# Moving the position terms into the q and k projection of a four-layer kernel, with earlier loads and an in-place norm

## The chip, the cores and the metric

The program runs on one core of a Trainium2 chip. The metric is the device time of one execution in microseconds; three runs of the kernel before are at hand, and one more execution was profiled. In what follows PE is the matmul engine, PEld its weight loads, DVE, ACT and POOL are the vector, scalar and general engines, and SP is the engine that issues most of the DMAs. A queue name such as SPq or ACTq means the issuing of a DMA by that engine.

## What is computed

The input is an image of 48 x 48 tokens with 768 channels, float32, and four layers follow each other. The first is an attention block with position terms:

```python
xn = layernorm(x)                                   # 2304 tokens, 768 channels
q, k, v = split(xn @ qkv_w + qkv_b)                 # 12 heads of 64
attn = (q * 64**-0.5) @ k.T
attn += rel_h[q_row, k_row] + rel_w[q_col, k_col]   # rel_h = q @ Rh(row), rel_w = q @ Rw(col)
x = x + softmax(attn) @ v @ proj_w + proj_b
x = x + gelu(layernorm(x) @ mlp_w1 + b1) @ mlp_w2 + b2
```

Layers two and four are spectral: a real 2-D Fourier transform, a two-layer block-diagonal complex network with soft shrinkage over the spectrum, the inverse transform, and the residual. Layer three is a scan: projections of the tokens give decay, angles and inputs, then 12 iterations of a depthwise 3 x 3 convolution of a state of 64 x 4 channels with injection, and an output projection with silu.

## The kernel before, in words

All matmuls are float32 except the position products, which use sums of three bf16 parts. The tokens are cut into six blocks of 384 (`TB`), two of which make a superblock `sb`; there are three. The large products are done with seven block products in place of eight (`combine`, `block_sums`, `rows_in_seven`).

The program is written in one order, and a scheduler reorders the instructions of each engine before the launch: an instruction later in the program may be put ahead when its inputs and buffers are ready in the scheduler's own timing. [...] A tile pool with `bufs=n` has n buffers of a tag; a new tile waits until a buffer is free. A pool that closes gives its space to later pools.

**qkv_phase (L181 to L461).** For each superblock: `prepare` norms two blocks of three 128-token tiles (`layernorm_rows`, L62, its last step at L84 into a tile `ln_xh`) and transposes them (L93) with copies by ACT and DVE (L95, L97) into `xnT`; `v_rows` computes v (L164); `q_and_k` goes over six pairs of heads `pr`, seven products each (L293), stores q and k through ACT's queue (L323) and reduces their maxima (L324). `load_qk` (L244) loads the pair's weights. `position_terms` gives 24 steps per superblock: 12 `rel_w` steps (L390) and 12 `rel_h` steps (L410), four matmuls each on a table `relD` that SP loads (L374), and a split into three bf16 parts by ACT and DVE in turn (L366 to L369). The results lie in the one tile `rw` and the one tile `rh`, 16 and 24 rows at a time are stored with six DMAs (L398) and, per block, four (L417). The steps of a superblock run between the products of the next superblock's v (`between`); those of the last one run after `ahead()`, that is after the loads of the first keys (L494), the first q chunk (L505) with its eight position loads (L472, L474), and the one-hot matrix (L480).

**attention_bounded (L514 to L615).** 36 chunks: six head pairs times six blocks of queries. In groups of three key tiles PE computes q-k products (L546), adds the position terms with the one-hot matrix (L554); ACT takes the exponential into tiles `p` (L556, nine buffers); DVE adds them up in `acc` (L561, L564); PE multiplies with the values (L575) one group later. `finish` sums `acc` over the keys with PE (L583), takes the reciprocal (L585) and scales (L586) with DVE. Every seventh group `weight_sums` (L721 onwards) does a piece of preparing later weights: loads into `p` tiles, sums on POOL, and stores (`second`, L752: the sums go to a tile of their own). Loads for the next chunk and pair are issued by SP.

**proj_phase, mlp_phase (L690, L772).** The projection and the MLP in seven products; rows of the norm are prepared within them. `follow` (L1474) takes each finished block of rows (half 0 or half 1 of the channels), loads it, transforms it (L1322) and stores it to `yu`; the last blocks are done after the last product with `last=True`.

**afno_first, scan_phase, afno_second.** `spectrum_mix` walks over 40 items (half, five columns, block) in four stages with a delay (L1380, L1394 to L1396, L1415/L1416, L1430); it begins with half 1. Then the inverse along the other axis, `f_w` (L1518). The scan's projections (L1061) run with activations (L1069 to L1081) and DVE work (L1089 to L1120) per three token columns; then 11 iterations over eight groups of channels (L1150 to L1170). At the end each group's product with the turned c (L1176, POOL) goes to the transposes (L1212). `afno_second` is the second spectral layer; its last loop (L1549 to L1552) adds the residual and stores the output through ACT's queue.

Of the kernel before, what the change touches and what calls it, by code (L numbers as in the profile page):

```python
# [11 lines left out]
F32 = mybir.dt.float32  # L12
# [7 lines left out]
P = 128  # L20
G = 48
# [40 lines left out]
def layernorm_rows(nc, pool, xt, name):  # L62
# [20 lines left out]
    xh = pool.tile([P, C], F32, tag="ln_xh", name=f"{name}_xh")  # L83
    nc.vector.tensor_scalar(xh, xt, mv[:, 0:1], r, ALU.subtract, ALU.mult)  # L84
    return xh
# [38 lines left out]
TERMS = ("T1", "T2", "T3", "T4")  # L124
# [56 lines left out]
def qkv_phase(tc, ident, x, qkv_w, qkv_b, relT, rel_d, ln_g, ln_b, q_d, k_d, v_d, rw_d, rh_d, wqk_d, wv_d, flag, ahead):  # L181
# [17 lines left out]
    with (  # L199
# [11 lines left out]
        def load_x(sb, half):  # L211
            for t in range(3):
                i = (2 * sb + half) * 3 + t
                Xs[i] = xp.tile([P, C], F32, tag="x", name=f"x_{i}", bufs=4)
                nc.sync.dma_start(Xs[i], x[i * P : (i + 1) * P, :])

        def prepare(sb, half):

            blk = 2 * sb + half
            if half == 0:  # L220
                ops[sb] = kp.tile([P, NC, 2, TB], F32, tag="xnT", name=f"xnT_{sb}", bufs=2)
# [45 lines left out]
        def q_and_k(sb):  # L267
            tok = slice(sb * TS, (sb + 1) * TS)
            q = qp.tile([P, NC, 2, TB], F32, tag="q", name=f"q_{sb}")
            made = []  # L270
            for pr in range(NC):
# [18 lines left out]
                for n in range(7):  # L290
# [28 lines left out]
                    else:  # L319
                        k_out(0, u)  # L320
                for o, d, m in ((q[:, pr], q_d, qms), (kt, k_d, kms)):
                    o = o.rearrange("p b t -> p (b t)")
                    nc.scalar.dma_start(d[pr * P : (pr + 1) * P, tok], o)  # L323
                    V.tensor_reduce(m[:, pr, sb : sb + 1], o, axis=AX.X, op=ALU.max, apply_absolute_value=True)  # L324
                if pr == NC2 and sb + 1 < NSB:
                    prepare(sb + 1, 0)
                    load_x(sb + 1, 1)
# [4 lines left out]
            return q  # L332
# [26 lines left out]
        with tc.tile_pool(name="qkv_o", bufs=1, side="right") as op:  # L359
            R = HD + G  # L360
# [16 lines left out]
            def position_terms(sb, q):  # L377

                q6 = q.rearrange("p c b (j w h) -> p c b j w h", j=KJ, w=KTW)
                rw = op.tile([P, 3, NC, TS], BF16, tag="rw", name=f"rw_{sb}")  # L380
                ds = {}

                def rel_w(g):

                    d = tables(1, g, sb)
# [5 lines left out]
                    at = rw.rearrange("p s c (b t) -> p s c b t", b=2)  # L391
                    cols = slice(j * P + w0 * KTH, j * P + (w0 + 4) * KTH)
                    split(ps[:R, :TB].rearrange("p (c b t) -> p c b t", c=NC, b=2), [at[:R, n, :, :, cols] for n in range(3)], f"w{sb}_{g}")
                    if g == G // 4 - 1:
                        for s in range(2):
                            for j in range(KJ):
                                r0 = s * HD + j * KTW
                                nc.sync.dma_start(rw_d[s, j, :, :, sb].rearrange("n w f -> w n f"), rw[r0 : r0 + KTW].rearrange("w n c t -> w n (c t)"))  # L398

                def rel_h(n, cp, hh):  # L400

                    blk = 2 * sb + n
                    if cp == 0:
                        ds[hh] = tables(0, 2 * blk + hh, 0)
                        if hh == 0:
                            ds["at"] = op.tile([P, 3, NC, TB], BF16, tag="rh", name=f"rh_{blk}")
                    ps = pm.tile([P, 512], F32, tag="m", name=f"rh_{blk}_{cp}_{hh}")
                    for i in range(4):
                        rhs = q6[:, 2 * cp : 2 * cp + 2, n, :, :, 4 * hh + i].rearrange("p c j w -> p c (j w)")
                        nc.tensor.matmul(ps[:R, i * 2 * G : (i + 1) * 2 * G], lhsT=ds[hh][:, i, :], rhs=rhs, start=True, stop=True)  # L410
                    at = ds["at"][:, :, 2 * cp : 2 * cp + 2].rearrange("p s c (w h) -> p s c w h", h=KTH)
                    split(ps[:R, :TB].rearrange("p (h c w) -> p c w h", h=4, c=2), [at[:R, k, :, :, 4 * hh : 4 * hh + 4] for k in range(3)], f"h{blk}_{cp}_{hh}")
                    if hh == 1 and cp == NC // 2 - 1:
                        for s in range(2):
                            for half in range(2):
                                r0 = s * HD + half * G // 2
# [1248 lines left out]
```

## Time and profile before

| what | value |
|---|---|
| median of three runs | 3935.67 us (3929.7 to 3935.88) |
| the profiled execution | 3932.65 us |
| its span, first to last instruction | 3930.7 us |
| granted TensorE clock, mean | 0.971 |
| PE busy / PEld | 3773.9 us (96%) / 2301.0 us |
| DVE / ACT / POOL busy | 2066.0 / 1116.4 / 649.0 us |
| moved by DMA | 457.24 MB, mean 116 GB/s |

By stages, with the time in which PE had a matmul:

| stretch (us) | what | PE busy | granted clock |
|---|---|---|---|
| 0 to 43 | first norm, first v | 23.2 | 0.88 |
| 43 to 468 | v, q and k, position terms | 420.0 | 0.99 |
| 468 to 553 | last position terms, first products of attention | 42.0 | 0.77 |
| 553 to 1730 | attention | 1163.7 | 1.00 |
| 1730 to 1864 | projection, norm | 129.6 | 0.98 |
| 1864 to 2881 | MLP | 1016.6 | 1.00 |
| 2881 to 2904 | between MLP and spectral layer | 5.0 | 0.61 |
| 2904 to 3163 | first spectral layer | 251.3 | 0.96, then 0.51 |
| 3163 to 3571 | scan | 394.5 | 0.98 |
| 3571 to 3652 | output of the scan | 71.4 | 0.74, then 0.97 |
| 3652 to 3931 | second spectral layer | 256.7 | 0.96, then 0.88 |

How to read it: the page of a profile gives the busy time of each engine, then the span in 40 equal slices (a digit is the busy share in tenths; PEclk is the clock granted to the matmul engine), the chain of work that ended last, and the costliest groups of instructions. A line of the chain in order of time is: start in us, duration in us, what. A line of the waits is: who waited, for whom, us in total, times, longest. A line of the timeline is: start, duration, engine, line of the kernel, operation, output and inputs with shapes, count, and in brackets the idle time before it and what ended it. A line of the windows is: the stretch, its length, busy time of PE, PEld, DVE, ACT and POOL with counts, the granted clock, the DMA share and GB/s. Float32 matmuls appear as two records each. Matmul ends are modelled in the profile.

### The profile page before, as it was taken

To read this page: it belongs to the slowest core of one execution; us is meant where nothing else is said; L and a number is where in the kernel's file an instruction comes from. 1 tells how busy PE (TensorE), PEld (TensorE's weight loads), DVE (VectorE), ACT (ScalarE), POOL (GpSimd) and SP (SyncE) were. 2 spreads that over 40 slices of the span, in tenths; PEclk is the share of its full clock that TensorE was granted. 3 is DMA by queue.
4 is the path that set the end of the run, shared out by engine and by line. 5 is a ranking of instruction groups with operands and counts; after the bars stand their busy time and mean duration, and the time that the engine had idled before them with its cause. 6 is when DMAs were issued, how large, how long until landed. Compare 5 with 4: busy or idle time off the path is not lost.

```text
span 3930.7 us, 54207 instructions
## 1 busy us (share of the span) xinstructions
PE 3773.9 (96%) x22018; PEld 2301.0 (59%) x22018; DVE 2066.0 (53%) x3184; ACT 1116.4 (28%) x1888; POOL 649.0 (17%) x497
## 2 busy tenths in 40 slices
PE   7999879999999999999999999999979998999998
PEld 4666544444444444445555555555558876996685
DVE  6645446666666666565425333232325357995345
ACT  1323234444444444420310120021013235222341
POOL 3101001011010101024000000000013210981131
PEclk9999989999999999999999999999989789999999
DMA  7666463333232322124334433533434302110444
GB/s 252 191 190 187 160 176 106 100 105 114 95 105 81 113 73 89 57 77 158 132 106 145 156 109 120 157 114 107 150 106 104 98 25 95 36 36 22 143 106 157
DMA packets 262426, 457.24 MB, mean 116 GB/s; under 512 B 32413, under 2 KB 215701, under 8 KB 255799
## 3 DMA queue, kind: packets, MB, share of 16 engines
q1 hardware_dynamic: 251927, 431.07, 36.1%
q10 hardware_dynamic: 10240, 22.61, 1.5%
q8 instruction: 175, 2.87, 0.3%
q14 instruction: 84, 0.69, 0.1%
HBM read 315.31 MB, written 138.31 MB: 115 GB/s over the span
## 4 chain that ended last, share of the span: by engine, by line
PE 81%; DVE 8%; DMA 4%; POOL 2%; issue 2%; ACT 2%; SPq 1%; ACTq 0%; DVEq 0%; POOLq 0%
PE p L845 12%; PE p L908 12%; PE av L575 10%; PE s L546 10%; PE qk L293 6%; PE s L554 4%; PE c L1061 4%; PE pj L164 3%; PE v L164 3%; DVE rec L585 2%; PE f_z L1415 2%; PE f_z L1416 2%; PE f_x L1380 2%; PE f_u L1430 2%; PE so L1221 2%
## 5 line engine op out<-in xcount | busy, mean ns | idle before, releaser
L564 DVE TENSOR_TENSOR acc<-acc,p 128x768 f32<-128x768 f32 x576 | 585.0, 1016 | 355.7 <-ACT p L556 314.0
L556 ACT ACTIVATE p<-s 128x768 f32<-128x768 f32 x648 | 478.4, 811 | 707.3 <-PE s L554 707.3
L546 PE MATMUL s<-qt,kt 64*128 64x384 f32 x2592 | 479.3, 502 | 22.5 <-DVE rest_h L367 21.1
L908 PE MATMUL p<-w,h 128*128 128x384 f32 x1512 | 492.4, 486 | 0.0
L575 PE MATMUL av<-p,vt 128*64 128x384 f32 x2592 | 467.4, 496 | 17.2 <-DVE oT L586 11.2
L908 PEld LDWEIGHTS p<-w,h 128*128 128x128 f32 x1512 | 286.4, 190 | 196.6
L546 PEld LDWEIGHTS s<-qt,kt 64*128 64x128 f32 x2592 | 233.7, 187 | 264.2 <-ACT p L556 88.2
L575 PEld LDWEIGHTS av<-p,vt 128*64 128x64 f32 x2592 | 172.2, 137 | 238.8 <-issue 194.0
L845 PE MATMUL p<-x2nT,w 128*128 128x384 f32 x864 | 293.8, 490 | 0.5 <-issue 0.5
L1150 PE MATMUL c<-H,bands 128*48 128x96 f32 x5632 | 242.6, 247 | 12.5 <-issue 12.3
L554 PE MATMUL s<-bt,oneh 120*128 120x384 bf16 x1296 | 248.7, 328 | 0.0
L1150 PEld LDWEIGHTS c<-H,bands 128*48 128x48 f32 x5632 | 235.5, 124 | 19.8 <-issue 12.7
L293 PE MATMUL qk<-xnT,wqk 128*128 128x384 f32 x756 | 244.8, 486 | 0.0
L845 PEld LDWEIGHTS p<-x2nT,w 128*128 128x128 f32 x864 | 165.4, 192 | 116.4 <-issue 3.2
L845 PE MATMUL p<-xT,w 128*128 128x384 f32 x648 | 220.8, 486 | 0.0
L554 PEld LDWEIGHTS <-oneh 120*128 120x128 bf16 x1296 | 109.3, 98 | 174.4 <-issue 113.2
L293 PEld LDWEIGHTS qk<-xnT,wqk 128*128 128x128 f32 x756 | 143.5, 190 | 99.3
L884 POOL TENSOR_TENSOR rr<-rr,ml_b 128x1152 f32<-128x1152 f32 x12 | 32.0, 2668 | 955.3 <-DMA rr<-xr_d 742.1
L840 ACT ACTIVATE h<-h,ml_b 128x384 f32<-128x384 f32 x144 | 88.4, 614 | 348.9 <-DVE h L860 176.6
L845 PEld LDWEIGHTS p<-xT,w 128*128 128x128 f32 x648 | 123.2, 190 | 85.8
L1158 POOL TENSOR_TENSOR t<-s,c 128x768 f32<-128x768 f32 x80 | 144.7, 1835 | 172.5 <-DMA bands<-in_bands_dram 160.6
L1061 PE MATMUL c<-wsc,x2T 128*112 128x357 f32 (+1 forms) x576 | 151.9, 427 | 2.0 <-DVE c L1022 2.0
(301 smaller groups left out, 4766.6 us busy)
## 6 DMA issues: line engine op xcount, KB each, us to landing
w<-w1s_d SPq DMA_DIRECT2D x36, 768.0 KB
w<-w2s_d SPq DMA_DIRECT2D x36, 768.0 KB
bt<-rh_d SPq DMA_DIRECT2D x144, 162.0 KB
w<-w1s_d SPq DMA_DIRECT2D x36, 576.0 KB
w<-in_mlp_w_dram SPq DMA_DIRECT2D x27, 768.0 KB
wqk<-wqk_d SPq DMA_DIRECT2D x12, 1344.0 KB
f_gt<-yu SPq DMA_DIRECT2D x24, 672.0 KB
bt<-rw_d SPq DMA_DIRECT2D x144, 108.0 KB
```

Source lines behind the costliest of these rows:

```text
L164: nc.tensor.matmul(p[:, :TB], lhsT=rhs[n][:, c, t * P : (t + 1) * P], rhs=w[:, c, :], start=c == 0, stop=c == NC2 - 1)
L293: nc.tensor.matmul(p[:, :TB], lhsT=w[:, n, c, :], rhs=ops[sb][n][:, c, :], start=c == 0, stop=c == NC2 - 1)
L546: nc.tensor.matmul(ps[:, s, :QB], lhsT=keys[pr][rows, kt * P : (kt + 1) * P], rhs=chunks[c][0][rows], start=True, stop=False)
L554: nc.tensor.matmul(ps[:, s, :QB], lhsT=oneh[:NBR, b % 3, :], rhs=chunks[c][1][:NBR, s, b // 3, j, :], start=False, stop=True)
L556: nc.scalar.activation(p, ps[:, :, :QB], AF.Exp)
L564: nc.vector.tensor_tensor(probs[c], probs[c], p, ALU.add)
L575: nc.tensor.matmul(avs[c][rows, :QB], lhsT=vals[pr][:, kt, rows], rhs=p[:, s, :], start=kt == 0, stop=kt == NT - 1)
L845: nc.tensor.matmul(p[:, :TB], lhsT=w[n][:, c, :], rhs=rhs[n][:, c, :], start=c == 0, stop=c == NC2 - 1)
L908: nc.tensor.matmul(ps[t][:, :TB], lhsT=hs[left, f][:, t * P : (t + 1) * P], rhs=wt[:, f % KW2, :], start=f == 0, stop=f == NF2 - 1)
L1061: nc.tensor.matmul(ps[:K, i, :n], lhsT=xT[:, cc, tok : tok + K], rhs=w[:, cc, c0 : c0 + n], start=cc == 0, stop=cc == NC - 1)
L1150: nc.tensor.matmul(ps[r0 : r0 + G, k // 4, cols], lhsT=bands[:, n - GC, i, :] if gr else bands0[:, n, i, :], rhs=H[:, n, :, d : d + NPR], ...
L1158: GP.tensor_tensor(t, sc[:, ch], c1[:, m0 : m0 + GC].unsqueeze(2).to_broadcast([P, GC, RR, NPR]), ALU.mult)
```

## The change

It has these parts.

1. The position steps come in another order, `rel_h` by pairs of q tiles first, and are called within the next products of the same superblock: two per pair `pr` from the third pair on (eight of 24), the rest between the products of the next v; in the last superblock four run after the bound and twelve after `ahead(1)`. Tables are loaded up to three steps ahead. The tables have 96 columns instead of 112, `rh` holds two q tiles for a superblock, and the stores are two DMAs per tile of 48 rows each.
2. Normed activations and keys with values share one pool `home`. The first keys and values and the one-hot matrix are loaded within the last superblock's q and k (`ahead(0)`), the first chunk where all loads stood before (`ahead(1)`).
3. `layernorm_rows` writes into its input; the x tiles have six buffers.
4. Attention: row sums and reciprocal are issued before the last group's values; ten `p` buffers; the sums of `second` are done in place and stored with two DMAs.
5. Rows of the spectral transform: the last MLP product has two calls of `follow`; the last block's rows are done in steps 1 and 4 of `spectrum_mix`.
6. The scan's activations come in another order; the last group's final product runs on DVE; the last output group of each half is stored in four DMAs on two queues; `gt` has three buffers.

```diff
-    xh = pool.tile([P, C], F32, tag="ln_xh", name=f"{name}_xh")
-    nc.vector.tensor_scalar(xh, xt, mv[:, 0:1], r, ALU.subtract, ALU.mult)
-    return xh
+    nc.vector.tensor_scalar(xt, xt, mv[:, 0:1], r, ALU.subtract, ALU.mult)
+    return xt
...
-                Xs[i] = xp.tile([P, C], F32, tag="x", name=f"x_{i}", bufs=4)
+                Xs[i] = xp.tile([P, C], F32, tag="x", name=f"x_{i}", bufs=6)
...
-                ops[sb] = kp.tile([P, NC, 2, TB], F32, tag="xnT", name=f"xnT_{sb}", bufs=2)
+                ops[sb] = home.tile([P, NC * TS], F32, tag="xn", name=f"xnT_{sb}").rearrange("p (c n t) -> p c n t", c=NC, n=2)
...
+                    if pr > 1 and n in (2, 5):
+                        step()
...
+                if pr == 1 and sb + 1 == NSB:
+                    ahead(0)
...
-            R = HD + G
+            R = 2 * G
...
+                def store(d, at, cols):
+                    for s in range(2):
+                        nc.sync.dma_start(d[s, :, :, sb, cols], at[s * G : (s + 1) * G].rearrange("k n c b t -> k n (c b t)"))
...
+                        tiles["rh"] = op.tile([P, 3, 2, 2, TB], BF16, tag="rh", name=f"rh_{sb}_{cp}")
...
+            def advance():
+                while len(ready) < 3 and steps:
+                    load, run = steps.pop(0)
+                    load()
+                    ready.append(run)
+                if ready:
+                    ready.pop(0)()
...
+            for _ in range(4):
+                advance()
             inner.close()
-            ahead()
-            for step in steps:
-                step()
+            ahead(1)
+            while steps or ready:
+                advance()
...
+    def keys_values(kv, pr):
+        nc.sync.dma_start(kv[:, :T], k_d[pr * P : (pr + 1) * P, :])
+        nc.sync.dma_start(kv[:, T:].rearrange("p (t c) -> p t c", t=NT), v_d[:, :, pr * P : (pr + 1) * P])
...
-        tc.tile_pool(name="at_q", bufs=2) as qp,
-        tc.tile_pool(name="at_p", bufs=9) as pp,
+        tc.tile_pool(name="at_p", bufs=10) as pp,
...
                 c, k0 = work[i - 1]
+                if k0 + KB == NT:
+                    row_sums(c)
                 for kt in range(k0, k0 + KB):
                     values(c, kt)
                 if k0 + KB == NT:
...
-            rhs = block_sums(nc, X, *(xp.tile([P, NC2, TB], F32, tag=f"x{n}", name=f"pj_x{n}_{sb}") for n in ("T1", "T2", "T4")))
+            rhs = block_sums(nc, X, *(sp.tile([P, NC2, TB], F32, tag=f"x{n}", name=f"pj_x{n}_{sb}") for n in ("T1", "T2", "T4")))
...
-        combine_right(nc.gpsimd, [i[n // 2][:, n % 2] for n in range(4)], *(o[:, n] for n in range(4)))
+        b11, b12, b21, b22 = (i[n // 2][:, n % 2] for n in range(4))
+        combine_right(nc.gpsimd, (b11, b12, b21, b22), b11, b22, b12, b21)
         yield
-        nc.sync.dma_start(w2s_d[:, :, f, :].rearrange("n p c -> p n c"), o)
+        for h in range(2):
+            nc.sync.dma_start(w2s_d[2 * h : 2 * h + 2, :, f, :].rearrange("n p c -> p n c"), i[h])
...
-                xt = xp.tile([P, C], F32, tag="x", name=f"ml_x_{blk}_{t}")
+                xt = xp.tile([P, C], F32, tag="x", name=f"ml_x_{blk}_{t}", bufs=6)
...
-                    if f == NF2 // 2:
+
+                    if f in ((3, 9) if (sb, n) == (NTB // 2 - 1, 6) else (6,)):
                         follow(psum)
...
-        follow(psum, last=True)
...
-                    nc.scalar.activation(ga, za[:, NA - 1 : NA, :], AF.Sigmoid)
-                    nc.scalar.activation(alq, za[:, NCR : NCR + NN, :], AF.Sigmoid)
+                    for t in (g, x):
+                        nc.scalar.activation(t, t, AF.Silu)
...
-                    for t in (c, x, g):
-                        nc.scalar.activation(t, t, AF.Silu)
+                    nc.scalar.activation(c, c, AF.Silu)
+                    nc.scalar.activation(ga, za[:, NA - 1 : NA, :], AF.Sigmoid)
+                    nc.scalar.activation(alq, za[:, NCR : NCR + NN, :], AF.Sigmoid)
...
-                    GP.tensor_tensor(by_q(hg[:K, nr]), by_q(Hd[:K]), crs[gr][:K].rearrange("p q n t -> p n q t"), ALU.mult)
+                    (V if gr == NG - 1 else GP).tensor_tensor(by_q(hg[:K, nr]), by_q(Hd[:K]), crs[gr][:K].rearrange("p q n t -> p n q t"), ALU.mult)
...
+            beside(step)
...
-    gt = pool.tile([YR, 4, TB], F32, tag="gt", name=f"{name}_gt_{half}_{g}", bufs=4)
+    gt = pool.tile([YR, 4, TB], F32, tag="gt", name=f"{name}_gt_{half}_{g}", bufs=3)
...
-        spectrum_mix(tc, "f1", a, "L1", yu, psum, True, "left", (1, 0))
+        follow = follow_in(gp, 1)
+        spectrum_mix(tc, "f1", a, "L1", yu, psum, True, "left", (1, 0), lambda step: follow(psum) if step in (1, 4) else None)
...
-                nc.scalar.dma_start(out[:, 4 * g : 4 * g + 4, cols], x3[:, 4 * g : 4 * g + 4, cols])
+                    if g == NTB - 1:
+                        (nc.scalar, nc.sync)[i % 2].dma_start(out[:, 4 * g + i, cols], dst)
+                if g < NTB - 1:
+                    nc.scalar.dma_start(out[:, 4 * g : 4 * g + 4, cols], x3[:, 4 * g : 4 * g + 4, cols])
```

## The prediction

> **What bounds the kernel now.** I read the page first: its busy row (PE 3773.9 us, 96% of the span) and the slices.
>
> ```profile
> PE   7999879999999999999999999999979998999998
> ...
> PEclk9999989999999999999999999999989789999999
> ```
>
> Every slice is 7 to 9, so only holes can be won: 3930.7 - 3773.9 = 157 us without a matmul, and the stretches at half clock. The fifth slice (393 to 491 us) and sixth hold the largest; the granted clock dips there too. The chain in order of time says what they are made of, the waits of PE who ended them:
>
> ```profile
> 473.66 9.42 DMA qt<-q_d
> ...
> 483.49 3.04 DMA relD<-in_relD_dram
> ...
> 520.12 5.96 DMA rh_d<-rh
> ...
> 539.79 9.49 DMA vt<-v_d
> 549.32 4.11 PE av L575 x12
> ```
> ```profile
> PE s L546 <- DVE rest_h L367: 21.1, 1, 21.1
> PE rw L390 <- DMA relD<-in_relD_dram: 11.5, 3, 10.8
> ```
>
> The q and k matmuls end at 467.9. PE then waits 10.8 us for a table queued behind the first chunk, and 21.1 us for the last split, itself late because the one buffer `rh` was being stored. Attention starts at 532.7 and stops again for the values until 549.3. Inside attention there is little:
>
> ```profile
> PE av L575 <- DVE oT L586: 11.2, 35, 1.3
> ```
>
> The next hole is between the MLP and the spectral layer, a chain of three transfers:
>
> ```profile
> 2878.36 3.01 DMA xa_d<-rr
> ...
> 2882.06 6.51 DMA f_x<-xa_d
> ...
> 2888.71 4.97 PE f_f L1322 x8
> ...
> 2894.34 3.81 DMA yu<-f_ys
> ...
> 2898.74 7.76 DMA f_yt<-yu
> ```
>
> From the timeline come the rest: scan start 12.3 us, scan end 8.9 us, end of the kernel 10 us, start 19 us.
>
> **The change, part by part.** Negative is time saved; the sum is made against the profiled execution, 3932.65 us, which is its span and 1.95 us around it.
>
> *Position terms within q and k, first keys and values early.* Eight of the last block's 24 steps move into its q and k: 8 x 1.40 us (one `rh` step in the chain), so q and k end at 467.9 + 11.2 = 479.1; nothing is saved by that alone. For the first two blocks the move is PE work for PE work, from v rows to q and k. It is covered by PE itself: DVE is busy 34.7 of 83 us in that stage and ACT 17.7, and a step costs them 1.1 and 1.0. The moved step brings its table load on SP (72 loads of 192 KB in place of 48 of 224) past the weight loads, where SP waits up to 13.1 us for PE; three tables are asked for ahead, some 20 us, which hides it. Stores fall from 14 to 8 a block, with the same bytes.
>
> After 479.1: the bound's reduction still holds PE 3.2 us, four `rh` steps end at 487.9. Their splits need `rh` back: the two stores of the step before are 0.86 MB; 1.3 MB took 9.95 and 5.96 us in the rows, so some 6 us, until 486. From there DVE paces it, two passes of 0.56 us a step: 16 steps end at 504 if no table is late. SP decides: if the first chunk's nine loads are issued at 484 (as in before, 5 us after the last matmul), 1.3 MB stands before the tables, not 2.5, and the wait is hidden. If they stand behind the third `rh` store, tables land near 500 and the steps end at 513; if they also wait for that store to land, 519. I take 511, nearer the middle, [...]: 532.7 - 511 = 21.7. The values are there: the first reciprocal came 48.7 us after the first product; a later chunk needs 38.9, less 2.9 for the missing chunk before it, and about 4 for half clock and the exp table: 40, so 8.7 more. Together **-30** (-37 to -20). The one-hot matrix is loaded with them. What is late next is the split on DVE.
>
> *Tables of 96 columns.* `rw` records are spaced 96.5 ns with weights of 112 columns; the spectral `f_z` records, 96 columns, 85 ns. 12 steps x 8 records x 2 blocks x 11.5 ns = **-2.2** (0 to -3). `rh` records, 175 ns, [...]: 0.
>
> *Norm in place, six x buffers.* Second-half norms no longer wait for the first half's transposes. At the MLP's start (1852 to 1864) PE waits 1.1 us for L84 and falls to half clock until 1870: **-3** (-6 to 0). At the third block's norm (219 to 234): 0.9 us and six matmuls at 4.1 instead of 2.0 us: **-2** (-5 to 0). At the start SP hangs 6.9 us on x buffers and holds up the weights that POOL combines; the bytes remain: **-2** (-4 to 0).
>
> *Attention.* Row sums move ahead of the last values. PE does the same matmuls, and the sums can wait for `acc`, 2 us ahead of need. But DVE is in order:
>
> ```profile
> 677.78 1.01 DVE L561 TENSOR_TENSOR acc<-p,p 128x768 f32<-128x768 f32 x1 [2.92 <-ACT p L556]
> 678.89 1.57 DVE L564 TENSOR_TENSOR acc<-acc,p 128x768 f32<-128x768 f32 x1
> 680.39 2.55 DVE L585 RECIPROCAL rec<-rs 128x384 f32<-128x384 f32 x1
> ```
>
> The row sums end at 679.6, yet the reciprocal starts when the next chunk's two adds end. They are ahead of it after the change too, unless the scheduler swaps them, so most of the 11.2 us stays. The in-place weight sums hold two more probability tiles until their store has landed; one tile is added. ACT waits only for PE in that stage. **-2** (-11 to +8, the latter 0.22 us in each of 36 chunks).
>
> *Last rows of the spectral transform.* The rows of half 1 move into the last product (3.06 us of PE either way), so the MLP ends at 2880.8 and the first `f_x` hangs only on its load, not on f_x, f_f and yu. The scan weights (1.8 MB) stand before it on SP if that load doesn't get ahead: 2.6 MB at about 250 GB/s from 2882 is 2892; ahead of them 2887. Before: 2903.95. -12, and the rows of half 0 now cost 8 x 0.33 = 2.6 us within the first items, where PE is full: **-9** (-16 to -3). Their load waits for xa_d on SP; behind it are y loads, three buffers ahead.
>
> *Scan.* Silu of g and x first: the first product starts 17.3 + 0.8 + 0.3 us instead of 21.7, but the sigmoids come last with a 1.28 us table load, and the sum H waits for them: 23.6 instead of 26.5, **-2.5** (-4 to 0). Within the projections PE is full and covers the order. The last group's product on DVE: POOL did two back to back (3.7 us); **-1** (-2 to 0), its table lands late anyway.
>
> *End.* Eight stores on two queues for two; in the last stretch DMA is full (share 1.04, 387 GB/s) and the bytes are the same, so the split gains little, and three g buffers for four can cost as much: **0** (-2 to +3). In the first spectral layer three are enough: at half clock a table lasts PE 5.1 us.
>
> *T tiles of the projection in a pool of their own, order of the T terms*: PE is full there (119.9 of 120 us) and hides both; without that cover, one DVE sum, 1.4 us.
>
> [...] Through the first spectral layer's last 63 us the granted clock is half, with PE never idle:
>
> ```profile
> 3120.00:3130.00 10.00, 10.00 (x48) 10.00 (x48) 1.67 (x3) 1.44 (x3) 0.17 (x1) 0.50 0.48 138
> ```
>
> [...] by the row it stays at 0.50 after the gap at 3097 to 3100, which the change leaves. I go by the row: 0.
>
> **Sum**: -30 - 2.2 - 3 - 2 - 2 - 2 - 9 - 2.5 - 1 = -53.7, so 3932.65 - 53.7 = 3879. The median of the runs, 3935.67, is 3.0 above the profiled execution: 3882.
>
> **Rivals.**
> - *The chunk's loads are late.* SP issues them behind the stores, or they wait for these to land, so tables and first products come at 519 or after, and the y load stands behind scan weights and slow: -20, -6, others as above: some -38, 3898. [...] Against: loads of `ml_x` at 1779 overtook stores to the same tensor's later rows. 0.25.
> - *More opens.* The scheduler lets reciprocals pass the adds (-9 more) and the y load pass the scan weights (-5 more): 3868. Against: the two adds' inputs come in the same microsecond. 0.12.
> - *The f_w phase keeps full clock*: -30 more, 3852. Against: the row. 0.03.
> - *Slower: probability tiles.* In 12 of the weight sums, seven groups each, four to six of ten tiles are held until the w2s_d store lands. If an exp is given such a slot, ACT stops, then PE. It takes 54 / 12 = 4.5 us a sum to cancel the gain; a landing of 6 us more than the scheduler's gives 72 us and 3954. Against: ACT's only waits are for PE, DMA is at 0.31, and four tiles cover a group. 0.04.
>
> **Numbers.** Likeliest case 0.56, 3882. The range 3856 to 3908 adds the unknown ends in quadrature (about 10 us of spread, twice that for 8 in 10) and takes in both neighbours. Within 0.2% of the median (7.9 us, about what a measurement of this kernel tells from no change) lies only a failed transition: 0.03. Faster 0.93, slower 0.04.
>
> **What would show it.** First product near 511, no wait for `vt`, and rec at 36 chunks 32.7 us apart: right. First product past 519, with `relD` or `rh_d` before it: the load order. First `f_x` about 11 us after the MLP's last matmul; f_w's clock 0.50; chunks above 33 us with ACT waiting for a DMA would mean the tiles. A granted clock of half in another stage would break the sum.

## The result and the profile after

The changed kernel takes 3900.05 us (median of four runs, 3896.0 to 3907.33) where the kernel before takes 3934.82: a ratio of 0.9916, 95% interval 0.9898 to 0.9934, so some 35 us less. On another chip, beside two later versions, it took 3907.59 (five runs, ratio 0.9935, interval 0.9921 to 0.9949), some 26 us less. The forecast was 3882 with a range of 3856 to 3908: the sign and the range hold, the size does not. About two thirds of the 53.7 us came in the first runs, half in the second.

The profiled execution has a span of 3893.8 us. The page's slices look nearly as before; the fifth and sixth are fuller:

```profile
PE   8999989999999999989999999999979998999998
...
PEclk9999999999999999999999999999989789999999
```

The waits of PE say more (who waited, for whom, us in total, times, longest):

```profile
PE f_x L1412 <- DMA f_yt<-yu: 18.2, 1, 18.2
...
PE pj L163 <- DMA pj_wt<-ps_d: 11.2, 1, 11.2
PE rw L400 <- DMA relD_w<-in_relD_dram: 11.0, 3, 9.7
...
PE qk L294 <- DMA wqk<-wqk_d: 5.6, 1, 5.6
PE f_w L1580 <- DMA f_gt<-yu: 5.2, 5, 1.3
PE s L556 <- ACT p L566: 4.7, 2, 3.2
PE p L860 <- POOL rr L899: 3.9, 1, 3.9
```

Gone are the wait for the last split (21.1), for the values (6.0) and all 35 waits of av for oT (11.2). New are 5.6 us for wqk, 5.2 for gt (0.3 before) and 3.9 at the MLP's start; the wait at the projection's start is 11.2 in place of 2.2. Behind the MLP there were two waits, 8.1 for the rows `f_x` from `xa_d` and 10.3 for y; now there is one, 18.2 for y. The wait for a position table has stayed: 11.5 in sum before, 11.0 after. Stage by stage, from first and last matmuls in the two profiles (the predicted column adds the terms of the prediction before they were rounded):

| stretch | before | after | measured | predicted |
|---|---|---|---|---|
| start to last q and k matmul | 467.9 | 479.1 | +11.2 | +5.0 |
| to the first product of attention | 64.8 | 34.4 | -30.4 | -32.9 |
| to the last matmul of attention | 1195.1 | 1176.6 | -18.5 | -10.7 |
| to the MLP's first matmul | 136.0 | 147.9 | +11.9 | -3 |
| MLP | 1016.7 | 1016.2 | -0.5 | 0 |
| to the first f_x | 23.3 | 18.2 | -5.1 | -12 |
| first spectral items | 196.6 | 198.1 | +1.5 | +2.6 |
| f_w, scan, its output | 550.8 | 548.2 | -2.6 | -3.5 |
| to the last transform | 234.8 | 230.3 | -4.5 | 0 |
| last transform to the end | 44.6 | 44.7 | +0.1 | 0 |

The rows that stand out most are attention, better than forecast by 8, and the stretch behind it, worse by 15. The q and k products and the first f_x are worse by 6 and 7.

### The profile page after: what moved, and what is told of

Read it like the earlier page. It is cut to its first block, busy times and chain, and to the rows that moved or that the text cites. A ratio compares the mean times of both kernels' runs of the same rounds, so it can differ in the third digit from the quotient of the medians.

```text
span 3893.8 us, 54463 instructions
## 1 busy us (share of the span) xinstructions
PE 3755.5 (96%) x22018; PEld 2283.2 (59%) x22018; DVE 2050.0 (53%) x3185; ACT 1141.6 (29%) x1907; POOL 654.2 (17%) x496
## 4 chain that ended last, share of the span: by engine, by line
PE 87%; DVE 5%; DMA 4%; ACT 2%; issue 1%; SPq 1%; POOL 1%; ACTq 0%; DVEq 0%; POOLq 0%
PE p L860 13%; PE p L923 13%; PE s L556 11%; PE av L585 11%; PE qk L294 6%; PE s L564 6%; PE c L1076 4%; PE v L163 3%; PE pj L163 2%; PE f_z L1447 2%; PE f_z L1448 2%; PE f_x L1412 2%; PE f_u L1462 2%; PE so L1237 2%; PE f_w L1549 2%; DVE s L1186 2%
## 5 line engine op out<-in xcount | busy, mean ns | idle before, releaser
L556 PE MATMUL s<-qt,kv 64*128 64x384 f32 x2592 | 477.7, 501 | 8.4 <-ACT p L566 4.7
L585 PE MATMUL av<-p,kv 128*64 128x384 f32 x2592 | 464.5, 493 | 0.0
L556 PEld LDWEIGHTS s<-qt,kv 64*128 64x128 f32 x2592 | 232.7, 186 | 248.8 <-ACT p L566 113.8
L585 PEld LDWEIGHTS av<-p,kv 128*64 128x64 f32 x2592 | 170.0, 136 | 225.2 <-issue 215.9
L1166 PE MATMUL c<-H,bands 128*48 128x96 f32 x5632 | 242.1, 247 | 11.7 <-issue 11.5
L1166 PEld LDWEIGHTS c<-H,bands 128*48 128x48 f32 x5632 | 234.1, 123 | 19.8 <-issue 11.9
```

Source lines behind the costliest of these rows:

```text
L556: nc.tensor.matmul(ps[:, s, :QB], lhsT=keys[pr % 2][rows, kt * P : (kt + 1) * P], rhs=qbs[qc % 2][0][rows], start=True, stop=False)
L585: nc.tensor.matmul(avs[c][rows, :QB], lhsT=vals[pr % 2][:, kt, rows], rhs=p[:, s, :], start=kt == 0, stop=kt == NT - 1)
L1166: nc.tensor.matmul(ps[r0 : r0 + G, k // 4, cols], lhsT=bands[:, n - GC, i, :] if gr else bands0[:, n, i, :], rhs=H[:, n, :, d : d + NPR], ...
```

## The experiments

Theory: what the change gave is what the rows say, and the missing part lies in places of its own: the projection's weights, the y load, and the wait for wqk. The rivals are named in each expectation. Ratios are to the kernel before on the same chip. Differences in us to "the changed kernel" are to its first median, 3900, unless said otherwise; its second median was 3908 on another chip, so a difference of less than 8 us between medians says little, and the stages decide. Norm in place, the narrower tables, the rows of the spectral transform and the scan's order were not run on their own; what is said of them is read from the stages.

**Row sums first: undone, and alone.** In the kernel before, the reciprocal stood behind two adds of the next chunk. The timeline of DVE after the change:

```profile
651.88 2.56 DVE L594 RECIPROCAL rec<-rs 128x384 f32<-128x384 f32 x1 [2.83 <-PE rs L592]
654.36 0.89 DVE L571 TENSOR_TENSOR acc<-p,p 128x768 f32<-128x768 f32 x1
655.17 0.54 DVE L600 TENSOR_TENSOR oT<-av,rec 128x384 f32<-128x384 f32 x1
```

DVE still waits 2.83 us here, but the reciprocal comes first when the wait ends, and the adds behind it. Two runs test whether that is the place of the row sums alone.

```diff
-                if k0 + KB == NT:
-                    row_sums(c)
                 for kt in range(k0, k0 + KB):
                     values(c, kt)
                 if k0 + KB == NT:
+                    row_sums(c)
                     finish(c)
```

> Edit: row sums and reciprocal go back behind the last group's values; all else is as in the changed kernel, with ten probability tiles. Theory 1 (place of the row sums): the 35 waits of av for oT come back, 11 us in sum, a chunk takes 33.0 us or so in place of 32.5: +11 us, some 3911. Theory 2 (something else in the change, the tenth tile above all, took these waits away): chunks stay at 32.5 us and the time at 3900.

Measured: 3921.84 us (ratio 0.9968, 0.9958 to 0.9978), 22 us above the changed kernel (14 above its second median). The waits are back, and longer than before the change:

```profile
PE av L585 <- DVE oT L600: 17.2, 34, 1.6
```

Theory 1 holds in kind. Its size was 11; from the first to the last row sum the stage takes 1153.0 us in place of 1134.7, 18.3 more. A wait for oT is 0.51 us here and 0.32 in the kernel before; why it is longer with the rest of the change is open. The other direction, the kernel before with `row_sums(c)` ahead of the values and nothing else:

> Edit: the kernel before, with this one part of the change alone: row sums and reciprocal are issued ahead of the last group's values. Theory 1 (the place of the row sums is the whole of it): the 35 waits of av for oT (11.2 us) go, a chunk takes 32.4 us in place of 32.8, and the time falls by 11 to 14 us against the kernel before, to some 3922. Theory 2 (the reciprocal still starts behind the next chunk's two adds on DVE, as I predicted, and needs another part of the change): the waits stay at 9 us or more, -2 us or less.

Measured: 3921.67 us (ratio 0.9962, 0.9948 to 0.9976), 15 us less than before. From the first to the last row sum it is 1134.7 us in place of 1146.9, 32.4 a chunk in place of 32.8, and no wait for oT is among the longer ones. Theory 1 holds: this one part gives 12 us in its stage and 15 in the medians.

**The projection's weights.** After the change SP issues them late (its timeline: start, us for issuing, line):

```profile
1620.73 0.40 SPq L496 DMA_DIRECT2D bt<-rh_d  x1
1690.12 0.41 SPq L103 DMA_DIRECT2D ln_g<-in_ln_g_dram  x1
...
1695.03 4.31 SPq L714 DMA_DIRECT2D pj_wt<-ps_d  x7
```

The queue issues nothing for 69 us, and then the MLP's parameters, whose space the keys and values hold until the last attention product at 1690.1; the weights stand behind them. In the kernel before they went out ahead of the parameters:

```profile
1665.10 3.51 SPq L700 DMA_DIRECT2D pj_wt<-ps_d  x7
...
1727.93 0.39 SPq L104 DMA_DIRECT2D ln_g<-in_ln_g_dram  x1
```

In the program's layout of on-chip memory (from the built program, not from a trace) `pj_wt` lies at 138,720 to 170,976 bytes of each partition. After the change the buffers of `attention_any`, the branch that these data never take, lie at 138,240 to 168,064; before, none of them lay there. The order of the queue is made ahead of the launch, for both branches, so a branch that does not run might hold a load back. The test lays two buffers of that branch elsewhere:

```diff
-                s = sp.tile([P, T], F32, tag="s", name=f"an_s_{h}_{t}")
+                s = kvs[0][:, (t % 2) * T : (t % 2 + 1) * T]
...
-                    pT = pp.tile([P, NT, GQ * P], F32, tag="pT", name=f"an_pT_{h}_{t}")
+                    pT = kvs[1].rearrange("p (t c) -> p t c", t=NT)
```

> Edit: two buffers of the attention branch that does not run on these data (its score rows and its transposed probabilities) are laid into the two key and value tiles, so that this branch ends below the place of the projection's weights. No instruction that is executed computes anything else. Theory 1 (place): the scheduler put the seven loads of pj_wt behind the MLP's parameters on SP because their space is shared with that branch; the parameters wait for the last attention product, so the weights came 11.2 us late. Then the loads now go out right after the last chunk's (some 60 us before attention ends), PE waits 1 to 2 us at the start of the projection in place of 11.2, and its first 36 records take 11.8 us in place of 14.1: 11 to 12 us less than the changed kernel, some 3888. Theory 2 (the tenth probability tile or the in-place weight sums hold the space): no difference, 3900, and the wait of 11.2 us stays.

Measured: 3895.08 us (ratio 0.9900, 0.9884 to 0.9917). The timeline of SP:

```profile
1623.85 0.40 SPq L496 DMA_DIRECT2D bt<-rh_d  x1
1627.72 3.54 SPq L714 DMA_DIRECT2D pj_wt<-ps_d  x7
1631.31 0.48 SPq L110 DMA_DIRECT2D pj_b<-in_proj_b_dram  x1
1693.28 0.39 SPq L103 DMA_DIRECT2D ln_g<-in_ln_g_dram  x1
```

PE's wait is 1.7 us in place of 11.2, and from attention's last matmul to the MLP's first it takes 137.2 us in place of 147.9. Theory 1 is shown in the stage: 10.7 us. The whole time fell by 5 us against the first median of the changed kernel and by 13 against the second (the profiled run had 3 us more in its first chunks and 4 more in the second spectral layer, see below).

**Steps moved into q and k.** The two calls per pair are left out, so that all steps run between the products of v or behind the last q and k.

```diff
-                    if pr > 1 and n in (2, 5):
-                        step()
```

> Edit: the changed kernel without the two position steps per pair within q and k; all steps of a block run between the products of the next v, those of the last block behind its q and k. Theory 1 (a step costs the same in either place, about 1.1 to 1.4 us): the q and k matmuls of the last block end 11 us earlier, near 468, and eight more steps follow them, which DVE paces at 1.1 us; first product of attention at 511 to 516 as now, 0 within 3 us. Theory 2 (behind q and k a step costs what it cost before the change, 61.7 us for 24 from the bound's end to the first product, 2.6 us each): eight steps cost 21 and save 11: first product near 523, +10 us.

Measured: 3904.96 us (ratio 0.9917, 0.9901 to 0.9934). The q and k matmuls end at 463.2, the first product of attention comes at 517.1, 3.6 us later than with the steps moved. The timeline of PE shows what the tail then waits for:

```profile
484.12 8.69 PE L412 MATMUL rh<-q,relD_h 128*96 128x96 f32 x48 [8.93 <-DMA relD_h<-in_relD_dram]
492.63 1.71 PE L398 MATMUL rw<-q,relD_w 128*96 128x96 f32 x16
500.10 6.25 PE L398 MATMUL rw<-q,relD_w 128*96 128x96 f32 x48 [5.75 <-DVE rest_h L369]
...
511.74 4.12 PE L398 MATMUL rw<-q,relD_w 128*96 128x96 f32 x24 [4.18 <-DMA relD_w<-in_relD_dram]
```

Theory 1, nearly: the move is worth some 4 us. The first product came at 532.7 before the change and comes at 517.1 without the move, so 15.6 of the 19.2 us by which it is earlier come from the other parts, the early loads, the new order and the stores among them; no run separates these. The wait for wqk is 2.6 us here in place of 5.6: the steps within q and k bring 3.0 of it.

**The y load.** SP's timeline after the change: the scan's weights wait there for the store `xa_d` (2855.1 to 2860.8), and the first y load stands behind them.

```profile
2855.11 0.42 SPq L908 DMA_DIRECT2D xa_d<-rr  x1
...
2860.86 0.39 SPq L1326 DMA_DIRECT2D wsc<-in_W_scan_dram  x1
...
2862.10 0.43 SPq L1385 DMA_DIRECT2D f_yt<-yu  x1
```

```diff
-        ... lambda step: follow(psum) if step in (1, 4) else None)
+        ... lambda step: follow(psum) if step in (1, 4) else load_wsc() if step == 8 else None)
```

(`load_wsc` is the load of the scan's weights, which no longer stands ahead of the layer.)

> Edit: the scan's weights (1.84 MB) are loaded in the ninth step of the first spectral layer's items, not ahead of them. Theory 1 (SP's order): in the changed kernel this load waits on SP until the store xa_d has landed (2855.1 to 2860.8), and the first y load, queued behind it, is issued 7.9 us after the MLP's last matmul and then shares the DMA engines with it; without it the y load goes out some 3 us after the last matmul and lands in 6 to 7: PE waits 9 to 11 us in place of 18.2, -8 us. Theory 2 (the y load waits for the landing of xa_d by itself, or the other loads fill the DMA engines): 15 to 18 us stay, -1 to -3 us.

Measured: 3897.98 us (ratio 0.9899, 0.9883 to 0.9916); PE waits 13.3 us in place of 18.2. The load was issued 4 us after the MLP's last matmul, as theory 1 said, and took 9.4 us to land, as theory 2 said: the DMA share is 0.98 in that gap. Each theory has half.

**The end.** Four gt buffers again, and one store for the last group again:

```diff
-    gt = pool.tile([YR, 4, TB], F32, tag="gt", name=f"{name}_gt_{half}_{g}", bufs=3)
+    gt = pool.tile([YR, 4, TB], F32, tag="gt", name=f"{name}_gt_{half}_{g}", bufs=4)
```

> Edit: four buffers for the spectrum tiles gt, as before the change, in place of three; the split store of the last groups stays. Theory 1 (buffers): the five waits for gt in the last transform (5.2 us) come from having three loads under way; with four they go, the last matmul comes 5 us earlier and the end too: -5 us. Theory 2 (bandwidth): the DMA engines are full there (share 0.95) and the bytes are the same; the waits go, the last matmul comes some 5 us earlier, and the stores end as late as now: 0, at most -2.

```diff
-                    if g == NTB - 1:
-                        (nc.scalar, nc.sync)[i % 2].dma_start(out[:, 4 * g + i, cols], dst)
-                if g < NTB - 1:
-                    nc.scalar.dma_start(out[:, 4 * g : 4 * g + 4, cols], x3[:, 4 * g : 4 * g + 4, cols])
+                nc.scalar.dma_start(out[:, 4 * g : 4 * g + 4, cols], x3[:, 4 * g : 4 * g + 4, cols])
```

> Edit: the last output group of each half is stored in one transfer on ACT's queue, as before the change; three gt buffers stay. Theory 1 (the split moved the end): from the last matmul to the end it takes 11 us again in place of 5.9: +5 us. Theory 2 (bandwidth): the DMA engines are full from the first gt load on, the stretch from the last transform's first matmul to the end stays at 44.7 us or within 2 of it, and the split only moved the last matmul: 0, at most +2.

Measured: 3904.74 us (ratio 0.9926, 0.9909 to 0.9942) and 3905.22 (0.9919, 0.9902 to 0.9935). From the first matmul of the last transform to the end it takes 45.1 us with four buffers, 44.5 with one store, 44.7 after the change and 44.6 before it. Theory 2 has the time in both, but not the way there. With four buffers the waits for gt don't go (one of 4.8 us in place of five, 5.2 in sum), and the last matmul ends 41.3 us into the stretch, not earlier than the 39.3 of the changed kernel. With one store it takes 5.4 us from the last matmul to the end, as with four, not 11. The stretch keeps its length while the last matmul ends anywhere from 33.7 us (before) to 41.3 into it. With a DMA share of 0.95 that speaks for the bytes as the limit; no run with fewer bytes was made.

```profile
3849.00:3889.00 40.00, 34.19 (x97) 15.47 (x95) 27.22 (x49) 0.00 (x0) 0.00 (x0) 0.96 0.95 332
```

(The windows of the changed kernel: busy PE, PEld, DVE, ACT, POOL, granted clock 0.96, DMA share 0.95, GB/s.)

**The half clock of f_w.** The prediction took the half clock of its row (0.50, with PE busy for 10.00 of 10.00 us) as given, with some 30 us at stake (an estimate: half of the 63 us that the phase took). The row was right for the change: the phase runs at 0.50 as before. Its start shows where the clock is lost:

```profile
3065.43 1.05 PE L1462 MATMUL f_u<-f_Z,f_ih 96*96 96x480 f32 x2 [1.44 <-DVE f_Z L1453]
...
3069.70 1.02 PE L1462 MATMUL f_u<-f_Z,f_ih 96*96 96x480 f32 x2 [1.53 <-DVE f_Z L1453]
```

PE stands idle for 1.44 and 1.53 us, the phase begins at 3070.6 with the clock still at 1.00, and at 3071.1 it falls to 0.50. In the second profile of the changed kernel the shortest record of f_w takes 367 ns (248 here, the median 421 in both): there the clock had fallen before the phase began. Two runs look into it. The first puts three unread matmuls of 384 columns into each of the last three steps of the items, so that PE isn't idle ahead of the phase:

```diff
+            if keep and step > len(items):
+                ps = psum(f"fill_{step}")
+                for i in range(3):
+                    nc.tensor.matmul(ps[:BS, :TB], lhsT=ih, rhs=ys[items[-1][:2]][0][:, i, :], start=True, stop=True)
             beside(step)
```

> Edit: three matmuls of 384 columns that nobody reads, in each of the last three steps of the first spectral layer's items, so that PE is not idle for 1.4 and 1.5 us right ahead of the inverse transform. The output is the same. Theory 1 [...]: without the gap the clock stays at full, and the inverse transform of 63 us takes 31 to 35: -28 us, some 3872. Theory 2 (the row: half clock belongs to this phase, however it is entered): the granted clock falls to 0.50 within the phase as it does now, and the added matmuls cost 1 to 3 us.

Measured: 3879.45 us (ratio 0.9861, 0.9845 to 0.9878), 21 us below the changed kernel. The timeline and the windows:

```profile
3078.67 32.30 PE L1553 MATMUL f_w<-f_iw,f_gt 100*128 100x96 f32 x288
```

```profile
3090.00:3111.00 21.00, 20.97 (x188) 20.80 (x187) 6.25 (x12) 5.74 (x12) 5.05 (x1) 1.00 0.90 271
```

The same 288 records take 32.3 us in place of 61.1, at a clock of 1.00: 28.8 us less, of which the added matmuls take back at most 2.5 (the items take 200.6 us; 198.1 and 199.2 in the two profiles of the changed kernel). The whole fell by 21 us against the first median of the changed kernel and by 28 against the second. Theory 1 against my reading. The second run leaves the idle time and puts ten such matmuls inside the phase, after three of its twelve tables:

```diff
+                if half and g == 3:
+                    ps = psum("mid")
+                    for i in range(10):
+                        nc.tensor.matmul(ps[:BS, :TB], lhsT=iw, rhs=gt[: 4 * KW, i % 4, :], start=True, stop=True)
```

> Edit: the changed kernel with ten unread matmuls of 384 columns within the first inverse transform, after three of its twelve tables; the idle time ahead of the transform stays. Theory 1 (hysteresis: the transform's own matmuls, 96 columns behind a weight load of 128, hold a full clock but cannot bring it back; longer ones can): the first three tables run at 0.50 as now (16 us), the ten take 7 to 12 us and the clock goes to 1.00 within them, and the other nine tables run at 1.00 in 24 us: the phase takes about 50 us in place of 63, -13 us. Theory 2 (only the idle time ahead decides, or the clock falls back after the ten): all tables take 5.1 us, the ten matmuls come on top: +8 to +12 us.

Measured: 3892.94 us (ratio 0.9895, 0.9878 to 0.9911). The timeline of PE:

```profile
3074.59 14.94 PE L1553 MATMUL f_w<-f_iw,f_gt 100*128 100x96 f32 x72
3089.32 8.09 PE L1549 MATMUL f_mid<-f_gt,f_iw 100*96 100x384 f32 x20
3097.25 16.21 PE L1553 MATMUL f_w<-f_iw,f_gt 100*128 100x96 f32 x144
```

72 records take 14.9 us ahead of the ten matmuls; 144, twice as many, take 16.2 behind them (72 more follow). From its start to the scan's projections the phase takes 49.3 us in place of 63.1: 13.8 less, as said. The granted clock is 0.50 until 3092.3 and 1.00 from there, 3.0 us after the first of the ten began. Theory 1: the phase's own matmuls held a full clock (1.00 for 32.3 us in the first run) but did not bring it back in 60 us; matmuls of 384 columns did in 3.0.

What it is in the phase's matmuls that does not bring the clock back is open, and their 96 columns alone are not it. In the kernel before, the clock fell at 3094.4 within an `f_u` of 480 columns and rose at 3097.9. From 3094.8 on PE ran only `f_z` there, records of 96 columns behind weight loads of 96. At half clock these follow each other every 0.16 us, those of f_w every 0.21.

**The changed kernel again, and two versions with more in them.**

> The changed kernel as it is, on the chip of the two combined versions. By its first runs (3896 to 3907, median 3900) and by its relatives that left its stages alone (3903 to 3905 with four gt buffers or one store), its time is 3900 to 3905, not the 3896 of its profiled execution; the 4.5 us that the second spectral layer seemed to save in that profile are then chance: here its items take 233 to 235 us from the scan's last output matmul to the last transform, as before the change.

Measured: 3907.59 us (ratio 0.9935), and 233.9 us from the scan's last output matmul to the last transform. The 4.5 us of the first profile in the second spectral layer are chance, as expected; the median was higher still.

The next version has the branch's buffers, the fill ahead of f_w, the late scan weights, and two edits more:

```diff
-            if i % 7 == 3:
+            if i % 7 == 3 and i > 3:
                 next(other, None)
...
-                    nc.sync.dma_start(wt[:, :n], w1s_d[f, :, 3 * i : 3 * i + n])
+                    (nc.sync if sb or f else nc.scalar).dma_start(wt[:, :n], w1s_d[f, :, 3 * i : 3 * i + n])
```

> Edit: together the branch's buffers (e1), the unread matmuls ahead of the inverse transform (e4), the scan's weights late (e6), the first piece of the weight sums one group of seven later, and the MLP's first weights through ACT's queue. Theory 1 (each works in its own place): -10 for the projection's weights, -20 for the clock, -5 for the y load, -3 for the stall of the first chunks, -4 for the MLP's start, in sum some -42: 3860 or less. Theory 2 (a transfer or wait behind each takes most of it back, as with the end): -20 to -25, only the clock's gain stays, 3878.

Measured: 3860.3 us (ratio 0.9822, 0.9800 to 0.9844), 47 us below the changed kernel on this chip; one of its five executions took 3879.96. Theory 1: the gains that the stages of the single runs showed (10.7, 26.3 and 4.9), with 3.6 in the first chunks, add to some 45. From the first product to the last row sum it takes 1171.2 us in place of 1174.8: the first piece's load had held SP for 8 us at 534.6 because it needed a probability tile, and the chunk's loads stood behind it. The MLP's start did not gain as said: 4.2 us of wait stay there, and its first weights, now on ACT's queue, go out at 1820.0, 7.4 us behind the projection's last matmul, where it was 7.2 on SP. The last version adds unread matmuls on the identity in the holes, six after each of the first two items, and the three at the end of the items in both spectral layers (the last two edits are left out below):

```diff
+def keep_warm(nc, ps, ident, n):
+    for i in range(n):
+        nc.tensor.matmul(ps, lhsT=ident, rhs=ident, start=True, stop=True)
...
+        keep_warm(nc, psum("warm")[:, :P], a["ident"], 40 if keep else 10)
         for step in range(len(items) + 4):
...
+                keep_warm(nc, pss[3][:, 1, half : half + P], ident, 40)
                 steps = [(it, gr) for it in range(1, ITERS) for gr in range(NG)]
...
+            keep_warm(nc, pm.tile([P, 512], F32, tag="m", name="so_warm")[:, :P], ident, 25)
             for p2 in range(NPR // 2):
```

> Edit: the version with all five, and unread matmuls (128 columns each, on constants) in four more holes: 40 between MLP and spectral layer, 40 ahead of the scan, 25 ahead of the scan's output, 10 ahead of the second spectral layer's items, 6 after each of the first two items and the three of 384 columns at the end of both layers. Theory 1 (a hole costs twice: its own length, and the half clock behind it): the first items, the scan's first groups, its first outputs and the second layer's first items run at full clock: 7, 4, 3 and 4 us less, some -16 against the version with all five. Theory 2 (what follows a hole is set by DVE, POOL or transfers, not by the clock): within 4 us of it; at worst the added matmuls stand in the way and it is slower by 3 to 6.

Measured: 3850.95 us (ratio 0.9791, 0.9778 to 0.9804), 9 us below the version with all five. But not where theory 1 put it: first items 199.3 us in place of 200.1, the scan 243 in both, its outputs 67.9 in place of 69.7. Of the 9.7 us between the two profiles 7.4 lie behind the last transform's first matmul (43.6 us in place of 51.0, at clocks of 1.00 and 0.76 to 0.85, with waits for loads of 4.4 and 7.0 us). But 51.0 is longer than in every other run (43.6 to 47.3), and the changed kernel itself takes 44.7 there, so most of the 7.4 belongs to that one execution and not to the filler. What the 9 us between the medians come from is open. Ahead of the first items the filler ran 9.2 us at full clock, and after 3.4 us of waiting the items still began at 0.60. Theory 2 is nearer.

## Why the prediction was partly right

*Position terms and first loads.* Right in its mechanism. Of the three load orders that it weighed the middle one came true, with the tables behind the third `rh` store ("tables land near 500 and the steps end at 513"):

```profile
492.28 1.21 SPq L389 DMA_DIRECT2D rh_d<-rh  x2
...
495.91 10.47 SPq L378 DMA_DIRECT2D relD_w<-in_relD_dram  x10
```
```profile
499.53 6.49 PE L400 MATMUL rw<-q,relD_w 128*96 128x96 f32 x48 [9.70 <-DMA relD_w<-in_relD_dram]
```

So a wait of 9.7 us for a table is still in this stretch. The first product came at 513.5 (511 said), 9.8 us ahead of the first product with the values, and no wait for the values is left. The q and k matmuls ended at 479.1, the number in the text, but by chance: the smaller terms, 6 us of gain, should have made it 473. They did come (the first q and k matmul 2.1 us earlier; in the third block's norm PE is busy 35.0 of 35 us, not 30.6; `rw` records 85 ns apart, and `rh` records still 175). A new wait of 5.6 us for wqk, not in my sum, took them back. I had said that three tables ahead "hides" the traffic of the tables; it hid it for the steps, not for the other loads on the queue.

*Attention.* The failed step is "They are ahead of it after the change too, unless the scheduler swaps them": it does, the adds come behind. The row sums now end at 651.8, just when the next chunk's first tiles `p` are being done (its first three exponentials run from 650.4 to 652.6). The rival "More opens" had this half, at 0.12. Where -2 stood (-11 as an end), this part alone gives 12 us in its stage of the kernel before and 15 in the medians. So -18.5 for the stage in place of -10.7, in spite of 3.2 us that the first chunk loses to the weight sums' load, a small form of the rival with the probability tiles.

*Behind attention.* The failed step is what is missing: no term for the start of the projection, which I held to be hidden because PE was full there, and -3 for the MLP's start, which I read from a wait of 1.1 us on L84. The first was a wait of 11.2 us in place of 2.2, and behind it the first 36 records took 14.1 us in place of 11.8. In the second the norm did get shorter: its transposes end 8.2 us behind the projection's last matmul in place of 11.1. But the MLP's first weights go out 7.2 us behind that matmul (7.6 before), and the first product comes 4.9 us after them (4.0 before), so PE waits for 3.9 us where it waited for 0.5. On SP these weights stand behind the last store of `xr_d`, but on ACT's queue they went out no earlier; what holds them is open.

*Last rows.* The failed term is the first f_x at "11 us" behind the MLP: 18.2. I had the scan weights ahead of it on SP, but not that they themselves wait for the landing of `xa_d`. And I counted 2.6 MB at 250 GB/s (an estimate; the kernel before moved 308 GB/s from 2882 to 2892 and 195 from 2889 to 2899), where 5.0 MB moved in this gap at 271 GB/s: the layer's tables, the store and two more y loads are beside them. Items +1.5 for +2.6.

*Scan, end.* -2.6 for -3.5 and +0.1 for 0: right, though both are as small as the differences between executions.

*Clock.* "I go by the row: 0" was right for this change. The reading of it was incomplete: what the row showed was a phase that loses its clock at its start, behind 1.44 and 1.53 us of idle PE, and did not bring it back by itself in 60 us.

*The sum.* It was missed by some 17 us in the profiled executions (-36.9 for -53.7). The largest misses are the projection's and MLP's start (15), the first f_x (7) and the wait for wqk (6); attention gave 8 back, and 4.5 of what was won in the second spectral layer was chance. The first rival's 3898 is close to the result by luck: its first product past 519 did not come, its slow y load did, and most of the loss lay where it had no term.

## What to carry to other kernels

Ask of every change in the layout of buffers which loads change places on their queue: a buffer that moves, even in a branch that isn't taken, can put a load behind a wait that it had nothing to do with (here a wait of 11.2 us in place of 1.7). When an instruction is issued earlier, look at what its engine was doing at the new time; here the reciprocal got ahead of two adds, for 12 us in its stage. A phase at half clock with PE full is worth a run with a few unread matmuls in or ahead of it before it is taken as given (here nine of 384 columns ahead took 28.8 us off the phase, ten within it 13.8).

## What the runs showed of the hardware

In this phase the granted clock depended on what ran before. The matmuls of f_w, 96 columns behind a weight load of 128 each, lost the full clock 0.5 us behind their start when PE had stood idle for 1.44 and 1.53 us just ahead, and then stayed at 0.50 for the rest of 61 us, though PE was busy for 58.00 of the 58.00 us from 3073 on; with matmuls of 384 columns in that idle time they ran at 1.00 for 32.3. Ten matmuls of 384 columns within the phase brought the clock back in 3.0 us. So in this phase it was not enough that PE had work; what in its matmuls makes the difference was not shown.

A hole filled with unread matmuls does not always help: 80 records of them ran 9.2 us at full clock, PE then waited 3.4 us for a load, and the granted clock was 0.60 in the 8 us behind it (2854 to 2862).
